# The order of finished rows in layer 2: rows of the first 17 node tiles before the others

## The chip, the cores and the metric

The kernel runs on one core of a Trainium2 chip. It is one program with one launch. The metric is the device time of an execution in microseconds. Before the change the median of three runs was 2305.02 us (2301.89 to 2305.65).

The engines are named as the profile names them: PE (TensorE's matmuls) and PEld (its weight loads), DVE (VectorE), ACT (ScalarE), POOL (GpSimd), SP (SyncE). Each takes its instructions in the order in which they stand in the program, and waits at an instruction whose inputs or buffers are not there.

## What is computed

Four graph attention layers over the same graph follow one another, each with a residual and a layer norm. There are 4096 nodes with 256 features; `adj` is 4096 x 4096, has about one entry in 256, and a full diagonal.

```python
x = _layernorm(x + _L0_gnn_ref(x, adj, ...))     # 4 heads of 64
x = _layernorm(x + _L1_gnn_ref(x, adj, ...))     # 4 heads of 64
x = _layernorm(x + _L2_gnn_ref(x, adj, ...))     # 2 heads of 128
x = _layernorm(x + _L3_gnn_ref(x, adj, ...))     # 1 head of 256, two softmaxes
```

Layer 2, for each head: `e = leaky_relu(s1[:, None] + s2[None, :])`, masked by `adj`, softmax over the neighbours, and the weighted sum of the neighbours' projected rows. Layer 3 does the same with the softmax of `e` and with the softmax of `-e`, weighs the rows of `x` by both, and multiplies the two results by `fc_W`:

```python
attention = softmax(where(mask, e, NEG_INF), axis=1)
negative_attention = -softmax(where(mask, -e, NEG_INF), axis=1)
h_prime_double = concatenate([attention @ x, negative_attention @ x], axis=1)
return elu(h_prime_double @ fc_W)
```

## The kernel before

**Node tiles and row tiles.** The 4096 nodes are 32 tiles of 128. A row tile m is the 128 rows of output of tile m. Since the graph is sparse, layer 0 packs the neighbours of each row tile into 13 gather tiles of 128 nodes (`NG`), with their indices in `idx` and the packed masks in `maskC`; the row tile's own nodes are a fourteenth position (`FRONT` = position 6). The first six gather tiles hold only nodes of the first 17 node tiles (`MIX` = 17, `NODES`), the other seven may hold any node.

**A row tile in layers 2 and 3** (`RowTile`). It has two halves of seven positions. `load(half)` issues the gathers of that half: six or seven indirect DMAs from GpSimd's queue (L630), which read rows of the DRAM tensor `vals` of the layer, and in half 0 also one plain DMA of the row tile's own rows (L627) from SyncE's queue. The gathers of half 0 read `vals[:17*128]`, those of half 1 the whole tensor. So a gather of half 0 waits until the rows of node tiles 0 to 16 have been written, a gather of half 1 until all 32 have. `half(half)` then makes the weights of seven positions and multiplies. In layer 2 these are L671 on ScalarE, L672 on VectorE and L683 on TensorE; in layer 3 seven L658, then L659 and L661 on ScalarE, L660 and L662 on VectorE, and L683. `finish(m)` divides, adds the residual, normalizes (L936 to L957, a chain of some twenty small operations on VectorE), stores the vector `y` (L959) and, up to layer 2, appends it to the list `ready` with the step from which it may be used.

The gathered rows lie in two pools of buffers, 16 for half 0 and 14 for half 1; in layer 3 a position takes one buffer, so two row tiles and a bit fit.

**Whole rows.** Layer 2 does 20 row tiles in this way and the last 12 (three blocks of four, node tiles 20 to 31) densely, over all 32 node tiles; layer 3 does 28 and 4. This is `whole_rows`: L901 and L902 in layer 2, L904, L906, L908 and L909 in layer 3 make the weights (`pw`), and L912 multiplies them with the rows `vw`. The block's edge terms `Sw` are four loads (L875), one for each of its row tiles. `whole(step)` deals these units out over the steps, so that the three blocks of layer 2 end at steps 11, 22 and 33 of 40.

**A step.** Row tile m and half `part` are step 2m+part. In layers 2 and 3 `half_with_whole` is one step: at most one projection of a finished row, one half of a row tile, the end of the row tile before, and some units of the whole rows.

**A projection** (`Projection`) makes the next layer's row of `vals` out of a finished `y`: two transposes on TensorE (L532), a copy `xT` on ScalarE (L537), the products (L546), the row's terms on ScalarE (L564) and VectorE (L566, L568, two L572), the DMA of the row (L574, 258 KB for layer 3, on SyncE's queue), a transpose of one term (L578), a copy of it (L584) and its DMA (L585) to the tensor `edge`, which the loads of `Sw` and of `S` read.

**Between the layers** `close` runs. It projects what is left in `ready` of node tiles below 17, loads half 0 of row tile 0 of the next layer, ends the last row tile, does half 0 of row tile 0, projects all the other rows that are left, and loads row tiles 1 to 3.

**Order.** The Python order is not the final one: a scheduler places the instructions of every engine into a fixed order when the program is built, by priorities that follow the Python order and by its own estimate of when inputs are ready. So a change in the order of projections also moves the instructions around them.

Of the kernel before, what the change touches and what calls it, by code (L numbers as in the profile page):

```python
# [76 lines left out]
MIX = 17  # L77
# [628 lines left out]
class Layer:  # L706
# [85 lines left out]
    def half_with_whole(self, m, part):  # L792

        proj = None
        self.step = 2 * m + part
        if self.ready and self.ready[0][0] < self.step:
            _, y, row = self.ready.pop(0)
            self.set_banks()
            proj = Projection(self.prog, self.n + 1, self.nxt, y, row)
            proj.transpose()  # L800
        if part == 1 or self.tile(m).accs is None:
            self.tile(m).half(part)
        if self.stored is not None:
            self.stored.store()
            self.stored = None
        if proj is not None:
            proj.copy()
            proj.multiply()
        if part == 1 and m >= 1:
            self.tile(m - 1).finish()  # L810
        self.whole(2 * m + part)
        if proj is not None:
            proj.row()
            proj.edge()
            self.stored = proj
# [643 lines left out]
```

## Time and profile before

| | us |
|---|---|
| median of three runs | 2305.02 |
| the profiled execution's own time | 2293.77 |
| its span, first to last instruction | 2292.0 |
| PE busy in the span | 2029.3 (89%) |
| PEld busy | 1847.6 (81%) |
| DVE busy | 1832.3 (80%) |
| ACT busy | 1752.1 (76%) |
| POOL busy | 1597.3 (70%) |

Three stretches of the span matter here:

| stretch, us from the span's start | what runs | PE busy | POOL busy | mean clock |
|---|---|---|---|---|
| 1318 to 1750 | layer 2, with the last halves of layer 1 | 406.31 of 432 | 305.08 | 0.98 |
| 1750 to 1800 | the end of layer 2, `close`, the start of layer 3 | 37.24 of 50 | 22.58 | 0.90 |
| 1800 to 2292 | layer 3 | 442.36 of 492 | 353.16 | 0.96 |

The first matmul of a row tile in layer 2 starts at 1355.5, the last of layer 3 at 2279.1. A line of a timeline reads: start in us, length in us, engine, source line, operation, output and inputs, how many were merged, and in brackets how long the engine stood idle before it and what the profile takes to have ended that. A wait for several semaphores is put down to the one that came last, so a named releaser can be another. TensorE runs each of these float32 matmuls as two passes, and the timeline counts passes.

### The profile page before, as it was taken

The page shows a single profiled execution, that of the slowest core. Times are in us where ns is not written, and L with a number is a line of the kernel's source. Part 1 is how long each engine was busy: PE and PEld are TensorE (multiplying, and loading weights), DVE is VectorE, ACT ScalarE, POOL GpSimd, SP SyncE. Part 2 cuts the span into 40 slices and gives each one's busy share as a digit, 9 for nine tenths or more (in the row PEclk, how much of TensorE's full clock was granted, in tenths as well). Part 3 has the DMA queues.
Part 4 walks back from the last instruction along what each step waited for, and adds up shares of the span by engine and source line. Part 5 has one row for each costly group of instructions (what it writes and reads, how often), then busy time and mean ns, then how long its engine had stood idle before and what let it go on. Part 6 is the DMA issues. An engine that isn't in the chain of part 4 may idle for free. (4 is left out here: it accounts for less than half of the span.)

```text
span 2292.0 us, 49763 instructions
## 1 busy us (share of the span) xinstructions
PE 2029.3 (89%) x15689; PEld 1847.6 (81%) x15689; DVE 1832.3 (80%) x6100; ACT 1752.1 (76%) x5137; POOL 1597.3 (70%) x1596
## 2 busy tenths in 40 slices
PE   4888998998998867999999898989998799979996
PEld 2667887888888767999888887989997688768885
DVE  2999999999987868999888886988976366655567
ACT  4779898997887758998888877988883667666663
POOL 2117887777787777777777777777761677777773
PEclk8989999999999988999999999999999899989998
DMA  8789788775455565666666556777764788888884
GB/s 279 257 259 337 228 265 272 258 262 179 136 154 157 151 203 163 189 187 170 179 167 184 168 153 186 221 203 235 230 199 140 249 263 266 267 252 273 264 251 133
DMA packets 250324, 492.00 MB, mean 215 GB/s; under 512 B 44385, under 2 KB 156610, under 8 KB 249666
## 3 DMA queue, kind: packets, MB, share of 16 engines
q0 software_dynamic: 81536, 245.30, 37.1%
q1 hardware_dynamic: 168514, 243.42, 32.8%
q8 instruction: 126, 2.06, 0.4%
q14 instruction: 148, 1.21, 0.2%
HBM read 436.24 MB, written 52.31 MB: 213 GB/s over the span
## 5 line engine op out<-in xcount | busy, mean ns | idle before, releaser
L630 POOL DMA_INDIRECT G<-vals,idx x1456 | 1584.3, 1088 | 654.1 <-issue 184.3
L671 ACT ACTIVATE w<-S,G 128x128 f32<-128x128 f32 x3248 | 994.0, 391 | 135.0 <-DMA G<-vals,idx 121.4
L680 PE MATMUL bank<-w,G 128*65 128x128 f32 x7168 | 845.5, 279 | 94.7 <-DVE w L668 71.7
L680 PEld LDWEIGHTS bank<-w,G 128*65 128x65 f32 x7168 | 809.4, 142 | 108.6 <-DVE w L668 87.7
L683 PE MATMUL bank<-G,w 128*128 128x257 f32 (+1 forms) x2688 | 496.8, 343 | 32.9 <-DVE w L672 10.4
L683 PEld LDWEIGHTS bank<-G,w 128*128 128x128 f32 x2688 | 437.4, 195 | 83.0 <-ACT z L971 11.6
L672 DVE SCALAR_TENSOR_TENSOR w<-w,mk 128x896 f32<-128x896 f32 x272 | 293.2, 1083 | 36.0 <-ACT w L671 33.9
L912 PE MATMUL bank<-vw,pw 128*128 128x129 f32 (+1 forms) x2048 | 302.2, 304 | 15.8 <-ACT zw L971 14.5
L912 PEld LDWEIGHTS bank<-vw,pw 128*128 128x128 f32 x2048 | 276.4, 193 | 33.0 <-ACT zw L971 14.9
L667 DVE TENSOR_SCALAR w<-S,G 128x128 f32<-128x128 f32 x896 | 238.3, 300 | 76.2 <-DMA G<-vals,idx 74.7
L658 ACT ACTIVATE w<-S,G 128x128 f32<-128x128 f32 x392 | 141.4, 391 | 138.0 <-DMA G<-vals 70.1
L430 DVE TENSOR_SCALAR oh<-iota,place 128x256 bf16<-128x256 f16 (+2 forms) x992 | 222.4, 301 | 8.5 <-PE bank L436 8.4
L672 DVE SCALAR_TENSOR_TENSOR w<-w,bank 128x896 f32<-128x896 f32 x192 | 206.3, 1081 | 8.8 <-ACT w L671 8.7
L436 PE MATMUL bank<-mk,oh 128*128 128x132 fp8e4 x2336 | 187.0, 225 | 14.9 <-DVE oh L430 10.5
L546 PE MATMUL bank<-wext,xT 128*128 128x268 f32 (+3 forms) x640 | 177.3, 408 | 21.6 <-ACT xT L537 18.1
L436 PEld LDWEIGHTS <-oh 128*128 128x128 bf16 x2336 | 143.1, 98 | 54.3 <-DVE oh L430 23.6
L909 DVE TENSOR_TENSOR pw<-pw,mw 128x512 f32<-128x512 f32 x64 | 44.0, 690 | 133.2 <-ACT pw L908 71.9
L546 PEld LDWEIGHTS bank<-wext,xT 128*128 128x128 f32 x640 | 116.6, 199 | 40.0 <-ACT xT L537 20.1
L373 ACT ACTIVATE mk<-raw 128x1024 uint8<-128x1024 int32 x128 | 131.7, 1063 | 17.2 <-DMA raw<-in_adjB_dram 16.7
L901 ACT ACTIVATE pw<-Sw,d 128x512 f32<-128x512 f32 x192 | 132.1, 714 | 14.8 <-PE bank L912 9.5
L902 DVE SCALAR_TENSOR_TENSOR pw<-pw,mw 128x512 f32<-128x512 f32 x192 | 127.6, 689 | 11.9 <-ACT pw L901 11.3
L443 ACT ACTIVATE cm<-bank 128x384 uint8<-128x384 f32 (+1 forms) x160 | 70.2, 450 | 56.4 <-PE bank L436 54.6
(131 smaller groups left out, 1716.3 us busy)
## 6 DMA issues: line engine op xcount, KB each, us to landing
raw<-in_adjB_dram SPq DMA_DIRECT2D x128, 512.0 KB
mk<-maskC SPq DMA_DIRECT2D x112, 224.0 KB
G<-vals,idx POOLq DMA_INDIRECT x1456
S<-edge SPq DMA_DIRECT2D x64, 256.0 KB
vw<-vals SPq DMA_DIRECT2D x96, 129.0 KB
xp<-y SPq DMA_DIRECT2D x96, 128.0 KB
y<-xp SPq DMA_DIRECT2D x96, 128.0 KB
mw<-maskW SPq DMA_DIRECT2D x20, 528.0 KB
```

The lines of the kernel that those rows point to most:

```text
L430: nc.vector.tensor_scalar(oh[:, :n * P], iota[:, :n * P], self.place[:, it, j:j + 1], None, op0=ALU.is_equal)
L436: nc.tensor.matmul(accs[b][:, s * MC:(s + 1) * MC], oh[:, (k - a) * P:(k - a + 1) * P], mk[:, j, it, :].bitcast(FP8), start=touches[b][0] ...
L546: nc.tensor.matmul(pp[:, :c1 - c0], self.xT[:, k, :], wext[:, k, c0:c1], start=(k == 0), stop=(k == KT - 1 and brow is None))
L630: nc.gpsimd.indirect_dma_start(out=self.place(pos), out_offset=None, in_=sh["v"][n][:NODES[t], :], in_offset=bass.IndirectOffsetOnAxis(ap= ...
L658: nc.scalar.activation(w[0][:, k, :], S[:, 0, :], AF.Relu, bias=d(k, 0))
L667: nc.vector.tensor_scalar(w[h][:, k, :], S[:, h, :], d(k, h), LEAST, op0=ALU.mult, op1=ALU.max)
L671: nc.scalar.activation(w[h][:, k, :], S[:, h, :], AF.Exp, bias=d(k, h))
L672: nc.vector.scalar_tensor_tensor(w[h], w[h], LEAST, mh, op0=ALU.max, op1=ALU.mult)
L680: nc.tensor.matmul(accs[0][:Wd, h * P:(h + 1) * P], v, w[h][:, k, :], **how)
L683: nc.tensor.matmul(a, w[h][:, k, :], v, **how)
L901: nc.scalar.activation(p, S[:, h], AF.Exp, bias=d)
L912: nc.tensor.matmul(accs[it][:, c:c + Wd], p[:, it, :], v[:, c:c + Wd], start=(j == 0 and h == heads[0]), stop=(j == NT - 1), skip_group_ch ...
```

## The change

It touches the choice of the row that a step of layers 2 and 3 projects; layer 3 has no next layer and its list is always empty. Before, the first entry of `ready` was taken if its step had come. After, all entries whose step has come are looked at, and those of node tiles below `MIX` = 17 come first; within the two groups the order of the list is kept.

```diff
         proj = None
         self.step = 2 * m + part
-        if self.ready and self.ready[0][0] < self.step:
-            _, y, row = self.ready.pop(0)
+
+        able = sorted((e for e in self.ready if e[0] < self.step), key=lambda e: e[2] >= MIX)
+        if able:
+            self.ready.remove(able[0])
             self.set_banks()
-            proj = Projection(self.prog, self.n + 1, self.nxt, y, row)
+            proj = Projection(self.prog, self.n + 1, self.nxt, *able[0][1:])
             proj.transpose()
```

An entry is (step, y, node tile). Nothing else is changed; `close` is the same.

## The prediction

> **What bounds the kernel now.** First the groups of instructions on the page, then GpSimd's own timeline, because the change touches what layer 3's gathers wait for.
>
> ```profile
> L630 POOL DMA_INDIRECT G<-vals,idx x1456 | 1584.3, 1088 | 654.1 <-issue 184.3
> ```
>
> ```profile
> 1706.03 1.14 POOL L630 DMA_INDIRECT G<-vals,idx  x1 [0.30 <-issue]
> 1762.60 0.94 POOL L630 DMA_INDIRECT G<-vals,idx  x1 [55.43 <-ACT pw L906]
> ...
> 1796.08 0.94 POOL L630 DMA_INDIRECT G<-vals,idx  x1 [7.48 <-DMA vals<-row]
> ...
> 1831.90 1.19 POOL L630 DMA_INDIRECT G<-vals,idx  x1 [1.18 <-PE bank L683]
> ...
> 2036.62 0.94 POOL L630 DMA_INDIRECT G<-vals,idx  x1 [3.96 <-PE bank L683]
> ...
> 2260.33 0.95 POOL L630 DMA_INDIRECT G<-vals,idx  x1 [0.30 <-issue]
> ```
>
> Layer 3 issues 28 x 13 = 364 gathers. Twenty go out from 1762.60, all for the first six gather tiles of row tiles 0 to 3, which read only rows of node tiles 0 to 16. Then GpSimd stands 7.48 us for a row write. From 1796.08 it issues the other 344 with two pauses, 1.18 and 3.96 us. The last starts at 2260.33, 464.3 us later: 344 x 1.335 us + 5.1. The span ends 30.7 us after it. So behind 1796.08 the layer runs at the pace of this queue, and **what counts is when gather 21 starts**. It reads rows of all node tiles, so it waits for the last row written, row tile 19's.
>
> The busy time per stage agrees: while GpSimd issues without a pause, TensorE runs full and later waits.
>
> ```profile
> 1840.00:1940.00 100.00, 99.81 (x461) 87.00 (x460) 58.00 (x176) 66.25 (x136) 76.95 (x76) 1.00 0.84 267
> 1940.00:2040.00 100.00, 80.48 (x355) 68.31 (x354) 60.55 (x184) 67.91 (x145) 74.71 (x72) 0.91 0.84 264
> ```
>
> (Columns: stretch; busy us and instructions of PE, PEld, DVE, ACT, POOL; clock, DMA share, GB/s.) Next SyncE's queue and ScalarE in the gap between the layers, which price the way to gather 21.
>
> ```profile
> 1757.15 0.38 SPq L875 DMA_DIRECT2D Sw<-edge  x1
> 1758.17 0.32 SPq L574 DMA_DIRECT2D vals<-row  x1
> ...
> 1790.38 0.32 SPq L574 DMA_DIRECT2D vals<-row  x1
> ```
>
> ```profile
> 1760.39 1.33 ACT L904 ACTIVATE pw<-Sw,d 128x512 f32<-128x512 f32 x2 [1.28 <-DMA Sw<-edge]
> ...
> 1767.64 0.40 ACT L658 ACTIVATE w<-S,G 128x128 f32<-128x128 f32 x1 [2.90 <-DMA G<-vals,idx]
> ...
> 1782.65 0.69 ACT L658 ACTIVATE w<-S,G 128x128 f32<-128x128 f32 x2 [0.16 <-DMA G<-vals,idx]
> ```
>
> Row 16's write is issued at 1758.17 and the first gather follows 4.43 us later; row 19's at 1790.38, and gather 21 follows 5.70 later. ScalarE has tile 0's first gather at 1767.64 (start of gathers + 5.04) and tile 1's last at 1782.65 (+ 20.05).
>
> **The change, part by part.** No instruction is added or removed: the same 32 projections run (six steps on the engines and two DMAs each), in another order. In the queue of layer 2, rows 20 to 31 came before rows 5 to 16 that finish at about the same time; now rows below 17 pass them. Counting steps (row tile m is finished at step 2m+3 and may be projected at 2m+5; rows 20-23, 24-27, 28-31 arrive at steps 11, 22, 33): before, rows 15, 28, 29, 30, 31 take steps 35 to 39 and 16, 17, 18, 19 are left to close(). After, 15, 28, 16, 29, 30 take them and 31, 17, 18, 19 are left. So **one** row, 16, moves ahead of the first gathers, and row 31 moves behind. GpSimd's order of gathers is the same but for one pair; the other engines' orders change near step 25, near the end of layer 2, and for nine groups of matmuls of the whole rows.
>
> (a) *Layer 2's body.* TensorE is busy 100.00 of 100 us in 1600 to 1700, so nothing is gained there. At step 25 row 10 is now asked for one step after it is finished. In the run of before its last normalizing operation ends at about 1641.97, and TensorE would reach its transpose at 1633.32 + 0.1 + 3.2 (28 passes) + 5.4 (48 passes) = 1642.0: no wait, 0. ScalarE then waits some 2.5 us for that product; its slack is the waits for TensorE that stand ahead of its L901s (0.17 us each, five per step) and 0.67 per step, and a step's weights are made a step ahead. I take 0, bounds 0 to +2.
>
> (b) *Gathers start earlier.* Up to 1738.39 TensorE's work is the same. Now 38 passes follow without a projection between: 38 x 0.1117 = 4.24, to 1742.63. Row 16's vector is ready at 1742.8 (before: 1742.37 + 0.41). Transpose and 6 passes to 1743.7, product 1.9 to 1745.6. VectorE takes the row after tile 18's chain, now uninterrupted, at about 1746.3; four operations take 0.9 (1757.21 to 1758.10 before), issue at 1747.3, gathers 4.43 later: **1751.7 for 1762.60, 10.9 us earlier.** Slots are free by then (tile 19's last matmul is at 1750.5). Bounds: landing 5.70 as row 19's, +1.3; vector +-1.
>
> (c) *What the early gathers drag along.* This is where the gain goes. In the changed order ScalarE has the activations of tiles 0 **and 1** (L658 to L661, which wait for the gathers) ahead of row 31's edge (L584) and of the copies xT of rows 17, 18, 19; before, tile 1's stood behind row 18's copy. ScalarE is in order, so all four rows wait for tile 1's last gather: 1751.7 + 20.05 = 1771.75. The last two L658 0.60, L659 0.84, L661 0.94: 1774.1. Edge of row 31: 1774.4.
> Then the whole rows' Sw, which needs that edge and whose exponentials stand ahead of row 18's and 19's terms: edge issue 1774.45, Sw issue 1.87 later (L585 at 1749.11 to L875 at 1750.98), ScalarE 3.24 later (1757.15 to 1760.39): 1779.55. Two L904 and one L906, 1.83: row 18's terms at 1781.5. Row 17's copy and product (1774.7 + 2.3 + 1.1) and row 18's (1778.1 + 2.3) are hidden under the Sw. Another four such activations, 2.43, the edge and xT of row 19 at 1784.55; product 2.0 to 1786.6, hidden under the next four (to 1787.0); row 19's terms 1787.15; one L909 0.65 and four row operations 0.9: 1788.6. **Row 19's write is issued at 1788.6 for 1790.38.** Landing: 4.43 or 5.70. Before, the 528 KB load of maskW was issued 0.83 us ahead of it and the last five gathers were still moving (DMA share 0.73); now that load stands behind the write and gather 20 is issued at about 1777, so I take row 16's 4.43: 1793.05 for 1796.08.
>
> Bounds of (c): tile 1's last gather after its issue took 6.06; the first took 5.04 and the tenth 7.10, so -1.0 to +1.0. Sw issue at most 2.7 (1754.44 to 1757.15), +0.8. Landing of row 19, +1.3. TensorE's clock: at 1790 to 1795 it was granted 0.50 after the wait before L578, and 28 passes took 8.47 us instead of 6.23; the changed order has TensorE waiting longer. Only row 19's product lies on the path then: up to +1.5.
>
> [...]
> [...]
>
> (d) *After gather 21.* Nine groups of four whole-row matmuls, 9 x 0.43 = 3.9 us, no longer fill the gap and lie in 1800 to 1860. TensorE waits for gathers from 1926.91 on (3.76 us the first time), so this cover takes them: 0; without it +3.9.
>
> **Sum:** 0 - 3.0 + 0 = -3.0: span 2289.0 for 2292.0. The profiled execution's own time was 2293.77, 1.8 beyond its span, and 11.3 below the median 2305.02; I put the difference on the median: **2302.0**. Worst of the bounds: +2 + 1.3 + 1 + 1 + 0.8 + 1.3 + 1.5 = +8.9; best -1 - 1 - 0 = -2: they seldom come together, so the forecast's own range is -5 to +3.
>
> **Rivals.**
> *Faster, by 5 to 10 us (2295 to 2300).* The pause before gather 21 goes almost wholly: 7.48 plus up to 2 if landings in the quiet gap are 4 us throughout and ScalarE gets tile 1 by + 18. For it: DMA share was 0.31 to 0.44 in 1750 to 1760. Against it: 20 gathers of 264 KB at 1.25 us are 211 GB/s by themselves, and the share in 1765 to 1785 was 0.83 to 0.97, so the burst is slowed by itself wherever it starts.
> *Slower: ScalarE's blocked queue.* Place: the L658s of tile 1 ahead of rows 17, 18, 19. Each us that tile 1's last gather is late is a us of the whole. It decides from + 23.1 on (no gain); at + 27.7 it is 4.6 us slower. With the clock's 1.5 and landings of 5.70 the turn comes at + 20.3 already. Price 5 to 9 us: 2310 to 2314. For it: own rows and row writes (258 KB each) share the same 20 us, and the rows behind ScalarE are now four instead of two. Against: the same own rows were in the measured burst.
> *The change does not do what it says.* Only row 16 moves, and the early gathers end in a longer stand before gather 21 (1777 to 1793, 16 us for 7.48): time 2303 to 2307. This is the forecast's edge and lies within it.
>
> **Chances.** A measurement of this kernel tells about 0.2% (4.6 us) from no change. Forecast and its edge 0.45, faster rival 0.31, slower rival 0.24. A little of each rival falls within 4.6 us and a little of the forecast outside: faster 0.33, same 0.43, slower 0.24. Range for 8 in 10: 2294 to 2311.
>
> **What would show it.** Right: first gather of layer 3 at 1750 to 1753; 20 gathers, then a stand of 13 to 18 us ended by a row write; ScalarE idle at L658 ahead of row 30's L564 and through tile 1's; row 31's L584 at about 1774; gather 21 at 1790 to 1796; 464 us from there to the last gather. Wrong: a gather 21 after 1798, a stretch from it to the end other than 495 us, or TensorE idle near 1642.

## The result, and the profile after

| | before | after |
|---|---|---|
| median, us | 2303.45 | 2299.99 |
| the single runs, us | 2300.0 to 2305.65 | 2298.14 to 2303.93 |
| ratio to before, 95% interval | | 0.9989 [0.9969, 1.0008] |
| the profiled execution: time, span, us | 2293.77, 2292.0 | 2298.14, 2296.4 |
| mean granted clock | 0.956 | 0.957 |

The median fell by 3.5 us; the interval reaches from 7.1 us faster to 1.8 us slower. The profiled execution of after has a longer span than that of before by 4.4 us, so the two profiles can't be compared end to end. Below, times are counted from row 15's transpose (in both orders rows 15 and 28 come one behind the other here; behind them the orders differ): 1725.9 in the profile of before, 1730.3 in that of after.

The groups on the page, and GpSimd's timeline of after:

```profile
L630 POOL DMA_INDIRECT G<-vals,idx x1456 | 1588.4, 1091 | 650.7 <-issue 180.0
```

```profile
1755.56 0.94 POOL L630 DMA_INDIRECT G<-vals,idx  x1 [45.47 <-PE bank L683]
...
1780.83 0.95 POOL L630 DMA_INDIRECT G<-vals,idx  x1 [0.30 <-issue]
1795.32 0.94 POOL L630 DMA_INDIRECT G<-vals,idx  x1 [13.55 <-DMA vals<-row]
...
2038.79 0.99 POOL L630 DMA_INDIRECT G<-vals,idx  x1 [4.94 <-PE bank L683]
...
2260.76 1.15 POOL L630 DMA_INDIRECT G<-vals,idx  x1 [0.30 <-issue]
```

The first gather comes 25.3 us after row 15's transpose; before it was 36.7. Of the 11.4 us won there, 6.1 go into a longer stand, the time that GpSimd idles in front of gather 21 (13.55 us for 7.48). Gather 21 comes 65.1 us after row 15's transpose, before 70.2. From it to the last gather it takes 465.4 us (464.3 before). Behind the last gather the profile of after takes 4.0 us longer, so from row 15's transpose to the end both have 566.1 us: in this pair of profiles the end shows nothing of what gather 21 gained.

The busy time in two stretches of layer 3 (columns as in the prediction) is about what it was:

```profile
1840.00:1940.00 100.00, 100.00 (x463) 87.55 (x463) 61.06 (x185) 68.83 (x145) 77.54 (x74) 1.00 0.86 266
1940.00:2040.00 100.00, 79.68 (x353) 67.88 (x352) 58.41 (x173) 65.06 (x140) 73.69 (x71) 0.93 0.85 264
```

SyncE's queue and ScalarE in the gap:

```profile
1779.58 0.32 SPq L877 DMA_DIRECT2D Sw<-edge  x1
...
1788.17 3.79 SPq L891 DMA_DIRECT2D vw<-vals  x2
1792.08 0.36 SPq L574 DMA_DIRECT2D vals<-row  x1
...
1794.61 0.32 SPq L889 DMA_DIRECT2D mw<-maskW  x1
```

```profile
1759.81 0.40 ACT L658 ACTIVATE w<-S,G 128x128 f32<-128x128 f32 x1 [2.85 <-DMA G<-vals,idx]
...
1774.28 0.98 ACT L658 ACTIVATE w<-S,G 128x128 f32<-128x128 f32 x3 [1.19 <-DMA G<-vals,idx]
...
1777.23 0.34 ACT L584 ACTIVATE erow<-bank,zero 1x128 f32<-1x128 f32 x1
...
1783.09 1.33 ACT L906 ACTIVATE pw<-Sw,d 128x512 f32<-128x512 f32 x2 [1.10 <-DMA Sw<-edge]
```

Here the predicted order can be read: tile 1's last activations at 1774.28, row 31's edge (L584) at 1777.23, the whole rows' Sw issued at 1779.58 and used at 1783.09, row 19's write at 1792.08. That write is followed by gather 21 after 3.24 us; before it took 5.70. The load of maskW (528 KB) stands behind the write now, and stood ahead of it before. What stands just ahead of the write now is a load of 129 KB (vw, the second of the two in that line, issued 0.43 us before the write).

### The profile page after: what moved, and what is told of

Its sections match the earlier page's. It is cut to its first block, busy times and chain, and to the rows that moved or that the text cites. A ratio compares the mean times of both kernels' runs of the same rounds, so it can differ in the third digit from the quotient of the medians.

```text
span 2296.4 us, 49752 instructions
## 1 busy us (share of the span) xinstructions
PE 2028.4 (88%) x15689; PEld 1850.6 (81%) x15689; DVE 1832.7 (80%) x6100; ACT 1746.6 (76%) x5137; POOL 1601.4 (70%) x1596
## 5 line engine op out<-in xcount | busy, mean ns | idle before, releaser
L680 PE MATMUL bank<-w,G 128*65 128x128 f32 x7168 | 846.3, 279 | 98.2 <-DVE w L668 69.0
L443 ACT ACTIVATE cm<-bank 128x384 uint8<-128x384 f32 (+1 forms) x160 | 70.2, 451 | 58.1 <-PE bank L436 56.2
```

Of the source, the lines that this page charges most:

```text
L680: nc.tensor.matmul(accs[0][:Wd, h * P:(h + 1) * P], v, w[h][:, k, :], **how)
```

## The experiments

The experiments ran in three groups, and the kernel before ran again in each. e5 to e8 ran on a chip like that of the first comparison (before: 2302.17 us). e1 to e4 and e9 to e12 ran on two chips where both kernels take 2800 us (before: 2808.13 and 2810.73), with a clock of about 0.88, so ratios are always to the kernel before of the same group. The kernel after ran again beside e2 to e4 (as e1) and beside e10 to e12 (as e9), not beside e5 to e8. There the engines stand still for nothing that the profile names: of the matmuls of layers 0 and 1, the page of the unchanged after in e9 has

```profile
L680 PE MATMUL bank<-w,G 128*65 128x128 f32 x7168 | 932.0, 288 | 199.5 <-issue 157.6
```

In the first profile of after that group took 846.3 us with 98.2 idle, most of it for VectorE's weights.

All profiles in one table, us from row 15's transpose. "Landing" is from the issue of row 19's write to the gather that waited for it.

| run | first gather | row 19's write | landing | gather 21 | gather 21 to the end | ratio to before |
|---|---|---|---|---|---|---|
| before | 36.7 | 64.5 | 5.70 | 70.2 | 496.0 | |
| e5, before again | 36.4 | 64.1 | 7.41 | 71.5 | 497.4 | |
| after | 25.3 | 61.8 | 3.24 | 65.1 | 501.1 | 0.9989 [0.9969, 1.0008] |
| e6, row 19 late | 25.1 | | | 72.4 | 499.5 | 1.0063 [1.0040, 1.0085] |
| e7, two a step | 29.6 | 57.6 | 3.38 | 61.0 | 497.2 | 0.9964 [0.9946, 0.9982] |
| e8, tiles 0 and 1 behind | 25.1 | 55.9 | 3.54 | 67.6 | 499.0 | 0.9976 [0.9961, 0.9991] |
| *the 2800 us chips:* | | | | | | |
| e1, after again | 25.1 | 64.2 | 3.20 | 67.5 | 546.1 | 0.9961 [0.9940, 0.9981] |
| e9, after again | 25.2 | 63.7 | 3.47 | 67.2 | 548.6 | 0.9972 [0.9949, 0.9996] |
| e2, end only | 25.2 | 63.2 | 3.14 | 66.4 | 555.8 | 0.9960 [0.9936, 0.9984] |
| e3, body only | 36.8 | 63.8 | 6.40 | 70.2 | 548.9 | 0.9992 [0.9965, 1.0018] |
| e4, tile 1 behind | 25.4 | 63.5 | 3.54 | 67.0 | 553.9 | 0.9979 [0.9957, 1.0001] |
| e10, two a step, tile 1 behind | 29.4 | 56.5 | 6.45 | 62.9 | 550.6 | 0.9970 [0.9943, 0.9997] |
| e11, two a step, old order | 34.0 | 62.8 | 5.03 | 67.8 | 545.8 | 0.9991 [0.9969, 1.0013] |
| e12, row 19 written again | 25.3 | | | 70.5 | 548.4 | 0.9988 [0.9962, 1.0014] |

In e6 and e12 gathers that don't need row 19 were placed behind gather 20, so the first one that needs it is number 23 in e6 (by the releaser that the profile names) and 26 in e12; in e8 it is number 15.

**e1, e9 and e5: both kernels again.** No edit.

> The changed kernel once more, unaltered. The profiled execution of after was 4.4 us longer in span than the profiled one of before (2296.4 against 2292.0), but 3.7 us of that are there at row 24's transpose (1626.56 against 1622.87), ahead of the first instruction that differs. Theory (the change is worth 0 to -4 us): ratio to before 0.998 to 1.000, and in the new profile gather 21 (the first gather that waits for row 19's write) comes 37 to 41 us after the first gather again (39.8 in after, 33.5 in before). Rival (the 3.7 us belong to the change, by the memory or the placement of code): row 24's transpose is again near 1626 and the ratio is 1.000 to 1.002.

> The changed kernel, unaltered, as the yardstick of this call. Expected: gather 21 64 to 66 us after row 15's transpose (65.1 in the first profile of after; 70.2 and 71.5 in the two of before), 496 to 501 us from there to the end, ratio to before 0.997 to 1.000.

> The kernel before once more (two empty lines keep the line numbers of after), for a trace under the conditions of these runs. Expected: against row 15's transpose the first gather of layer 3 comes 36 to 37 us later and gather 21 70 us later, as in the first profile of before; in the changed kernel these were 25.3 and 65.1 (67.4 in its second profile).

The first gather and gather 21 come about where expected in both kernels on the first kind of chip (gather 21 at 71.5 for 70 in e5). On the 2800 us chips they miss by a little: in e1 gather 21 comes 42.4 us after the first gather (37 to 41 expected), in e9 67.2 us after row 15's transpose (64 to 66 expected). From there to the end e9 takes 548.6 us, where the 496 to 501 of the first kind of chip had been expected. The ratio of e1 is better than expected, that of e9 at the edge, and both intervals leave out 1. The 3.7 us by which row 24's transpose came later in after's first profile aren't the change's: the second profile of before has it at 1618.9, and e7 and e8, which are the same program as after up to step 33, at 1619.9 and 1631.0. So 11 us of difference come and go in the first 1630 us.

**e2 and e3: the two halves of the change.**

```diff
-        able = sorted(..., key=lambda e: e[2] >= MIX)
+        able = sorted(..., key=lambda e: self.step > 33 and e[2] >= MIX)    # e2
+        able = sorted(..., key=lambda e: self.step < 34 and e[2] >= MIX)    # e3
```

> Only the second half of the change: from step 34 on the rows of node tiles below 17 go first, before that the list is taken in its old order. It leaves row 16's move out of the closing stretch as it is and takes away the exchange in steps 25 to 33. Theory (all that counts is row 16's move, and the exchange near step 25 costs 0.7 us for row 10's wait at its transpose): first gather 10 to 12 us earlier against row 15's transpose than in before (36.7 us behind it there, 25.3 in after), gather 21 and the end as in after or 0.7 us before it: ratio to before 0.997 to 0.999. Rival (the exchange near step 25 helps, since the terms of early rows come sooner): slower than the changed kernel by over 1 us.

> Only the first half of the change: rows of node tiles below 17 go first up to step 33, from then on the old order, so that row 16 stays in the closing stretch with 17, 18 and 19. Theory: the first gather stands where it stood in before against row 15's transpose (36.7 us behind it), gather 21 too (70.2 us behind it in before), and the time is that of before plus 0 to 0.7 us: ratio 1.000 to 1.001. Rival (the exchange near step 25 is where the 3.5 us of the median come from): ratio 0.998 to 0.999.

The second half alone has the ratio of the whole (0.9960 and 0.9961, side by side), the first half alone none that can be told from 1. In e3 the first gather and gather 21 stand exactly where before has them. What moves gather 21 is row 16's move (and row 31's). That the exchange near step 25 costs 0.7 us, as in the profile of after, is below what these times resolve.

**e4 and e8: take the early activations out of the way.** In e4 row tile 1's S, in e8 those of tiles 0 and 1, take part in one VectorE operation with row 19's terms, so that their activations come behind it; in e8 tile 0's half also moves behind the last projections.

```diff
+            proj = Projection(self.prog, self.n + 1, self.nxt, y, m)
+            proj.all()
...
+            s, t = following.tile(1).S, proj.terms          # e8: tiles 0 and 1
+            self.nc.vector.scalar_tensor_tensor(s[:, 0, :], t[:, 0, 0:1].to_broadcast([P, P]), 0.0, s[:, 0, :],
+                                                op0=ALU.mult, op1=ALU.add)
             following.tile(1).half(0)
```

> The changed kernel, and layer 3's row tile 1 can't begin its activations before row 19's terms are there (one VectorE operation adds zero times a term of row 19 to its S). So ScalarE has only tile 0's seven activations ahead of row 31's edge and no longer waits for tile 1's gathers (1770.91 to 1776.29 in after) in front of the copies of rows 17, 18 and 19. Theory 1 (ScalarE's queue behind tile 1's gathers holds rows 17 to 19): row 19's write and gather 21 come 3 to 6 us earlier than in after. Theory 2 (TensorE holds them: tile 0's 28 matmuls of 7.29 us at 1768.28 stand in front of row 31's transpose anyway, which ends at 1775.7): row 31's edge copy moves only from 1777.2 to 1775.8 and gather 21 by 1 to 2 us. In both, the end follows gather 21 by no more than half if the stretch from 1826 to 1926, where TensorE has no gap, takes the rest back: ratio to the changed kernel 0.998 to 1.000 under theory 2, 0.997 to 0.999 under theory 1.

> The changed kernel with layer 3's row tiles 0 and 1 both held back until row 19's terms are there, so that rows 31, 17, 18 and 19 have ScalarE and TensorE to themselves. Theory (tile 0's activations, and its 28 matmuls of 7.3 us on TensorE in front of row 31's transpose, hold the last four rows): row 19's write 8 to 12 us earlier than in after. But tile 0's buffers then come free only some 10 us after that write, and gathers 15 to 20 wait for them, so gather 21 is no earlier than in after by more than 2 us, and the time is after's within 3 us. Rival (the four rows are a chain of their own of 4.5 us each): row 19's write moves by less than 3 us, gather 21 comes 8 to 12 us later, and the time grows by 4 to 10 us.

e4 bears out its second theory for row 31's edge, which comes 45.9 us after row 15's transpose (47.3 in e9). Row 19's write (63.5 for 63.7) and gather 21 (67.0 for 67.2) move by less than the 1 to 2 us that it named. TensorE has tile 0's matmuls in front of row 31's transpose:

```profile
2217.17 6.59 PE L683 MATMUL bank<-G,w 128*128 128x257 f32 x28
```

They end at 2223.8, 45.1 us after row 15's transpose, so row 31's edge can't be earlier by more than it was. The whole rows' Sw is used 1.9 us earlier than in e9 (52.8 us for 54.7). That was lost again on TensorE, whose granted clock was 0.50 from 2234.95 to 2238.37: six passes of the whole rows that stand in front of row 19's product took 2.58 us there, and 1.47 in e9.

```profile
2236.11 2.58 PE L920 MATMUL bank<-vw,pw 128*128 128x257 f32 x6
```

With both tiles out of the way (e8) row 19's write comes 6.0 us earlier than in after: less than the 8 to 12 expected of the theory, more than the rival's 3. What is left to hold it stands on ScalarE:

```profile
1781.56 1.33 ACT L912 ACTIVATE pw<-Sw,d 128x512 f32<-128x512 f32 x2 [7.54 <-DMA y<-xp]
1782.80 0.15 ACT L564 ACTIVATE row<-bank 128x2 f32<-128x2 f32 x1
```

L912 is the whole rows' first weight (L906 in after). It stands ahead of row 18's terms (L564) and waits 7.54 us; the profile names another load, but its input is Sw, whose last load was issued at 1777.11, 5.8 us after row 31's edge was (1771.35). So a second stop stands behind the first: taking one away uncovers the other. The buffers of tile 0 come free later here (its matmuls start 62.3 us after row 15's transpose, in after 38.0), gather 15 already waits for row 19 (16.84 us, by the releaser that the profile names), and gather 21 is 2.5 us later than in after, as expected. By the ratios the time was some 3 us under after's (0.9976 against 0.9989, in different groups), which the intervals don't resolve.

**e6 and e12: is it gather 21?** e6 has sixteen multiplications by one on GpSimd, e12 two more writes of row 19 from GpSimd's queue, all in front of the first gather that needs row 19. The fence has both edits in one: e6's lines stand ahead of the row's own write, e12's behind it.

```diff
+        if n == 3 and m == 19:
+            for _ in range(16):
+                nc.gpsimd.tensor_scalar(row[:, :64], row[:, :64], 1.0, None, op0=ALU.mult)         # e6
+            for _ in range(2):
+                nc.gpsimd.dma_start(out=sh["v"][n][m * P:(m + 1) * P, :], in_=row)                  # e12
```

> The changed kernel with sixteen more operations on GpSimd on the first 64 columns of row 19, between gather 20 and gather 21 of its queue, where GpSimd only waits. They multiply by one, and row 19's write waits for them: gather 21 comes later by their length d, read from the trace, and no other engine gets work. Theory (the start of gather 21 sets the end, all other things follow it): the time grows by 0.8 to 1.0 d. Rival (after gather 21 TensorE's backlog of whole-row groups gives half of any shift back, as it seemed to do between 1826 and 1926): it grows by 0.3 to 0.6 d. A third (the stand is hidden altogether): by less than 0.2 d.

> The changed kernel, and row 19 is written twice more to the same place from GpSimd's queue, each write behind the one before. GpSimd's order puts the gathers of row tile 3 that don't need row 19 between them, so the first gather that needs it is not number 21 but number 25 or so; counted back by the gathers ahead of it (1.25 us each), gather 21 comes 4 to 9 us later than in after. No engine but GpSimd's queue has more to do, and that only waits there. Theory (the end keeps its distance of 496 to 501 us from gather 21, counted so): the time grows by 0.7 to 1.0 of that shift, 3 to 9 us. Rival (the shift is hidden behind TensorE's work after it): under 2 us.

In e6 gather 23, where the profile names row 19's write, starts 75.0 us after row 15's transpose, in after gather 23 starts at 67.9: d = 7.1 us. The end comes 572.0 us after the transpose, in after 566.1: 5.8, or 0.8 d. The last gather comes 9.1 us later than in after; 3.4 us of that at most are the slower gathers described next (10 ns for each of 343), so at least 5.7 us, again 0.8 d, are left there. But the time grew by far more (1.0063 against 0.9989, 17 us), and that is no measure of d: every gather of e6 takes longer, from the start of the program on. All gathers from 300 to 1700 us, shortest, median and longest in ns:

```profile
L633 POOL DMA_INDIRECT G<-vals,idx x985: 951/957/4297, 299.9 to 1699.3; - x197
```

In after the same gathers have 940, 947 and 4297. Ten ns by 1456 gathers are 15 us at most.

e12 has no such effect (949 ns; the kernel after on the same kind of chip 949). Its waiting gather, number 26, comes 78.5 us after row 15's transpose, 73.5 and 74.1 in e9 and e1: 4.4 to 5.0 us later. The end comes 618.9 us after it, 615.8 and 613.6 there: 3.1 to 5.3 us later. But the end is no measure here: in e2, with the same rows in the closing stretch, it comes 622.2 us after the transpose without any delay, since the stretch behind the last gather varies by more than the shift (30.5 to 39.0 us in e1, e9, e2 and e12). The last gather is a better one: 587.9 us in e12, 584.6, 583.1 and 583.2 in e9, e1 and e2, so 3.3 to 4.7 us later. So e6 agrees with the theory and with neither rival; e12 agrees with it as far as the last gather, and by their times e12 and e9 can't be told apart.

**e7, e10 and e11: two projections a step.** From step 34 on a step projects a second row if one is ready; e10 adds e4's edit, e11 has the list's old order.

```diff
+        if self.step > 33 and len(able) > 1:
+            self.ready.remove(able[1])
+            proj.store()
+            self.stored = None
+            self.set_banks()
+            Projection(self.prog, self.n + 1, self.nxt, *able[1][1:]).all()
```

> The changed kernel, and from step 34 on a second projection in a step where a second row is ready, so that rows 29, 30 and 31 need not wait for later steps or for the closing stretch. Theory 1 (the projections run one behind the other at 4 to 5 us each, from row 28's on, and the steps were not what held them): row 19's write and gather 21 within 1.5 us of after's place against row 15's transpose (65 to 67 us), the first gather 3 to 8 us later than there, the time that of after within 1 us. Theory 2 (the closing stretch is filled up by rows that a step could have taken): gather 21 6 to 10 us earlier, the time 3 to 9 us less than after.

> Two projections in a step from step 34 on, as in the run before, and row tile 1's activations held back until row 19's terms are there. With two a step gather 21 came 61.0 us after row 15's transpose and GpSimd still stood for 5.3 us before it, since row 19's copy xT waited on ScalarE behind tile 1's activations (1773.5 to 1777.4). Theory (ScalarE's order in front of row 19 is the last thing between gather 20 and gather 21): row 19's write 3 to 5 us earlier, the stand 0 to 2.5 us, gather 21 56 to 58.5 us after row 15's transpose, the time 2 to 5 us less than with two a step alone (ratio to before 0.994 to 0.9955). Rival (tile 1's matmuls, now later, hold up the buffers of gathers 22 and on, or the whole rows' first weights, which wait for Sw, take the place on ScalarE): within 1.5 us of two a step alone.

> Two projections in a step from step 34 on, with the old order of the list: row 16 comes behind rows 28 to 31, ahead of 17, 18 and 19, all in one chain of 4.2 us each. Theory (the order of the list is worth what gather 20 gains over gather 21, so it counts only if row 19 is early enough): the first gather 4 us later against row 15's transpose than with two a step and the new order (29.6 there), 33 to 34.5; gather 21 at 59 to 63 us, the time within 3 us of two a step with the new order. Rival (the early first gather is the whole gain): gather 21 later by the same 4 us, 64 to 66, and the time 4 us more.

In e7 the first gather is 4.3 us later than in after, as its first theory had it; row 19's write and gather 21 are some 4 us earlier, on the second theory's side but not by its 6 to 10. The stand has shrunk:

```profile
1784.60 1.10 POOL L630 DMA_INDIRECT G<-vals,idx  x1 [5.29 <-issue]
```

This is the best version on that chip, 0.9964, and better than before. Whether it beats after can't be said from times: the two did not run side by side there, and the intervals overlap.

e10 missed its expectation. Its stand is 4.66 us instead of 0 to 2.5. On ScalarE the whole rows' weights took the place of tile 1's activations ahead of row 18's edge:

```profile
2231.42 1.32 ACT L918 ACTIVATE pw<-Sw,d 128x512 f32<-128x512 f32 x2
2232.64 0.34 ACT L584 ACTIVATE erow<-bank,zero 1x128 f32<-1x128 f32 x1
```

Row 19's write is still earlier by 1.2 us than in e7 (56.5), but its landing takes 6.45 us. SyncE's queue shows what stands ahead of it:

```profile
2236.62 0.38 SPq L901 DMA_DIRECT2D mw<-maskW  x1
2237.43 0.32 SPq L574 DMA_DIRECT2D vals<-row  x1
```

e11 goes beyond its rival at gather 21: 67.8, 4.9 us behind e10 and 6.8 behind e7, though row 31's edge and Sw are early. With two a step the order of the list is worth 5 to 7 us at gather 21, with the reserve that e10 has e4's edit too and e7 ran on another kind of chip. At the end nothing of it can be read: from row 15's transpose to the end e10 and e11 have 613.5 us each, and the intervals of their ratios overlap.

## Why the prediction was right, point by point

**The sum.** Predicted -3.0 us, measured -3.5 (medians), and -0.28% to -0.39% on the other chips. Over the three comparisons the change gains some 0.1 to 0.4%, so it lies on the border of what was called no change. That -3.0 and -3.5 lie so close is in part luck: the interval of the measured change is 8.9 us wide, and at gather 21 the profiles show 5.1 to 6.4 us instead of 3.0. The text's reason, that the end follows gather 21, held on the first kind of chip within some 5 us: over its six profiles gather 21, by its number in the queue, ranges from 61.0 to 72.4 us after row 15's transpose, while the time from it to the last gather stays within 463.7 to 467.8, and that to the end within 496.0 to 501.1. On the 2800 us chips the tie is looser (545.8 to 555.8 to the end), and GpSimd makes 25 to 30 pauses of over 1 us behind gather 21, where on the first kind of chip it makes one or two. There the medians of after lie 7 to 9 us under before, with gather 21 only some 3 us earlier (against e3). Where the rest of that gain comes from stays open.

**(a) Layer 2's body: 0.** Small, as said, but not nothing. Where the prediction had no wait at row 10's transpose, TensorE waits 0.32 us in after:

```profile
1646.08 0.41 PE L532 MATMUL bank<-ident,y 128*128 128x128 f32 x2 [0.32 <-DVE b L957]
```

From row 24's transpose to row 15's it takes 103.7 us for 103.0. That lies within the bounds given, and e3's time can't tell it from 0.

**(b) First gather.** Predicted 1751.7, that is 25.8 after row 15's transpose; 25.3 in after, 25.1 to 25.4 in all runs with the changed closing and one projection a step.

**(c) What is dragged along.** The steps came in the order named, each a little early (from row 15's transpose, predicted and measured): row 31's edge 48.5 and 47.0, Sw's use 53.7 and 52.8, row 19's write 62.7 and 61.8, gather 21 67.2 and 65.1. Two things in it were off.

The mis-sized term is the landing of row 19's write: taken at 4.43 us, a gain of 1.3. It was 3.24. Sorted by what stands ahead of the write, the twelve profiles in which the landing can be read fall into two groups: where the 528 KB load of maskW is issued 0.8 to 1.5 us ahead of it, 5.03 to 7.41 us (before, e5, e3, e10, e11); where it stands behind or isn't near, 3.14 to 3.54 (after, e1, e2, e4, e7, e8, e9). In these seven the queue isn't empty either: the load of 129 KB is issued 0.4 to 0.7 us ahead of the write. SyncE's lines of before in e5, and gather 21 followed at 1793.45:

```profile
1785.20 0.32 SPq L889 DMA_DIRECT2D mw<-maskW  x1
1786.04 0.32 SPq L574 DMA_DIRECT2D vals<-row  x1
```

The traces' DMA records show when the packets move: the write's first moves 0.87 to 1.08 us after its issue in the seven, and 1.98 to 2.98 us after it in the five, where the load's packets move first (in before from 0.11 to 3.70 us, the write's from 1.98 to 4.36). The other reason that the prediction named, gathers still moving, can be told apart in one pair: in before and in e7 gather 20 is issued 2.7 and 2.9 us ahead of the write, and the landings are 5.70 and 3.38. With gathers issued closer to the write, or behind it, the slow landings range from 5.03 to 7.41, so the gathers may add to them.

So of the gain at gather 21, 2.5 to 4.2 us go with a load that fell behind the write, about as much as the earlier write brought, or more (2.7 and 2.3 us in after; on the 2800 us chips, against e3, the write comes between 0.6 us earlier and 0.5 later in e1, e2 and e9, so there the landing is nearly the whole gain). The prediction had this load in its text as a reason for the smaller of two landings, and priced it too low. No run moved that load alone, so the split is read from the profiles, not tried, and why the write's packets come late behind that load is shown by no run.

The other thing is the holder. The prediction let all four rows wait for tile 1's last gather. e4 took that wait away and gather 21 moved by 0.4 us at most: TensorE's matmuls of tile 0 stand in front of row 31's transpose as well, and what Sw gained was lost to TensorE's clock. And e8 shows that Sw, which the prediction had as its next step, is a stop of its own.

**(d) Nine groups moved behind gather 21: 0.** Right as far as it can be read: from gather 21 to the last gather 465.4 us in after, 464.3 and 465.8 in the two profiles of before.

**What the span has besides.** 3.7 us upstream, which come and go (e5, e7, e8). And 4.0 us behind the last gather's start: 35.6 us for 31.7 (the prediction's 30.7 counts from that gather's end). With them gather 21 is 501.1 us from the end, and a stretch other than 495 us was one of the prediction's own signs of being wrong. What differs is when the last 98 passes start: 4.2 us ahead of the last gather in before, 0.9 us ahead of it in after, 2.6 us behind it in e2, whose tail (from the last gather's start to the end) was 39.0. The lines of before, after and e2:

```profile
2256.10 23.36 PE L683 MATMUL bank<-G,w 128*128 128x257 f32 x98 [6.56 <-DVE z L990]
```

```profile
2259.83 24.14 PE L683 MATMUL bank<-G,w 128*128 128x257 f32 x98 [6.44 <-DVE z L992]
```

```profile
2764.14 24.02 PE L683 MATMUL bank<-G,w 128*128 128x257 f32 x98 [11.48 <-DVE z L992]
```

They wait for VectorE's end of an earlier row, in before as long as in after, so the length of that wait doesn't explain the 4.0 us. The long tail isn't in every run of the kernel: e1 and e9 have 30.5 and 31.2. But all tails of over 33 us (after, e7, e2 and e4) belong to the new order, and that it has no part in them isn't shown.

**The clock.** In after TensorE's granted clock is 0.50 from 1763.45 to 1770.28, right behind a wait of 4.14 us. Row 31's product took 3.81 us there (2.01 elsewhere) and tile 0's 28 passes (14 matmuls in the program) 7.29 us (6.23 at full clock): 2.9 us more. ScalarE reached row 31's edge only after that (1777.23, behind tile 1's activations and without a wait), so here it cost nothing. Row 19's product took 1.90, at a granted clock of 1.00: it fell behind whole-row matmuls, and the up to 1.5 us that the bounds of (c) put on it weren't paid in after. In e4 1.1 us were paid, in the six passes in front of that product.

**The rivals.** The slower one was to decide if tile 1's last gather came later than 23.1 us after the first; it came at 18.7. The faster one needed the stand to go; it grew to 13.55. The third, a longer stand, is what happened, and left a small gain.

## What to carry to other kernels

When work is moved ahead of a queue's last wait, price what else the move reorders: here a load's move behind the deciding write went with about as much (2.5 us off the landing in after) as the write's earlier issue brought (2.7). A stop taken away uncovers the next (behind tile 1's activations tile 0's matmuls, then the whole rows' first weights, which wait for Sw, in e8 7.54 us), so follow the chain to the instruction that the end waits for. And compare two profiles from a common instruction, not from the start: what lies ahead of it (11 us between two profiles) and behind the last gather (31.7 us in before, 35.6 in after) differed by more than the 3.5 us by which the median fell.

## What the runs showed that was not expected

- The same write of 258 KB lands in 3.14 to 3.54 us with a load of 129 KB issued just ahead of it, or in 5.03 to 7.41 behind one of 528 KB on the same queue.
- On two chips the kernel before takes 2808 and 2811 us for 2302, with idle time that nothing in the profile explains; the distances in the closing stretch are within some 2.5 us of those on the first kind of chip.
- Sixteen operations on GpSimd near the end of the program went with gathers that took 957 ns (median) instead of 947 from its start on. This was one kernel and one profile, and the cause is open.
